# Rewriting the written order of a two-layer convolution kernel, with the first pair's norms taken chunk by chunk

## The chip, the cores and the metric

The kernel runs on one core of a Trainium2 chip. The metric is the device time of one execution in microseconds (us), the median of several runs.

## What is computed

Two layers act on an image `x` of shape (4, 128, 128, 128): 4 images, 128 channels, 128 x 128 pixels. Cut to what matters:

```python
def _block(x, ...):                       # t: one row of 128 channels for each pixel
    t = _ln(t, ln0_g, ln0_b)
    y1 = _ln(t, ln1_g, ln1_b)
    t = t + einsum(sigmoid(y1) * y1, W_out)
    y2 = _ln(t, ln2_g, ln2_b)
    wht = einsum(y2, W_whiten)
    k = square(relu(einsum(wht, W_key)))  # 512 hidden channels
    kv = einsum(k, W_value)
    r = sigmoid(einsum(wht, W_recep))
    return t + r * kv

x = x + _block(_gn(x)) + transposed(_block(transposed(_gn(x))))   # layer 0
x = x + conv3x3(_gn(x), weight[0]) + bias, scaled by a gate per channel   # layer 1
```

The block works on each pixel by itself, so its two calls give the same, and the kernel computes it once and adds it twice. `_gn` is a group norm over 4 channels and a whole image, `_ln` a layer norm over the 128 channels of a pixel. The gate of layer 1 comes from the mean of each channel of the normed image.

## The kernel before

**Tiling.** Channels lie on the 128 partitions. An image is cut into 32 chunks of 512 pixels; two chunks are a pair (16 pairs an image, 64 in all), four chunks a block of 16 rows (8 blocks an image, 32 in all). Twelve blocks are held in SBUF, and both layers write into them in place.

**Layer 0, one pair.** Each step is a word in the order, with the norm or chunk in its digits. In the names below `h` is the chunk of the pair, `j` the quarter of the hidden channels:

- `u` (L674, ACT) applies the group norm, `Tu` (PE) turns a chunk so that pixels lie on the partitions, 4 tiles of 128 x 128.
- `bn0h` (L685, DVE) takes the statistics of 4 tiles, `nb0` (L727) makes 1/std and -mean/std of them for all 8 tiles of the pair: six small steps, a power of -0.5 (L718, always on POOL) and two small steps. `t` (L735, ACT) applies them. `g` and `b` (L740, L744, POOL) are gain and shift.
- `bn1h`, `nb1`, `z1h` (ACT), `Tz1h` (PE) are the second norm and its way back to channels on partitions; `silu` (ACT), `att` (PE, 4 matmuls a chunk), and `T` (DVE) add the attention term to `t`.
- `bn2h`, `nb2` give the third norm's 1/std. `rc` (L771, DVE) turns it, `W` (L777) stores it in DRAM with four DMAs, `R` (L783) loads it for a chunk, spread over all partitions. `tt` (PE) turns `t` back and `cp` (L797, DVE) multiplies it with `R`.
- `pk` (L808, PE), `re` (ACT), `sq` (ACT, or DVE where the table FIRST_SQUARES has a D; from PSUM then), and `kv` (PE) are key, relu, square and value for `j` = 0 to 3; `pr`, `th` (ACT) the receptance; `q` (DVE) and `x` (POOL) gate and add, `S` (DVE) adds `t`, `bx` (DVE) takes the statistics for layer 1.

The power and the small steps belong to three words: `sa` the six steps, `pw` the power, `nb` the rest. For pairs under EARLY (2) the list has all three, with the small steps on DVE; for the others `nb` issues everything on POOL.

**Layer 1, one block.** The convolution is done by rows in a form with six products (`c0` to `c5`, L872, three matmuls each): DVE makes their inputs (`p`, `q`, `p2`, `q2`, `v0a` to `v5b`), and DVE and ACT combine the results (`e1`, `e3` on ACT; `a`, `b`, `c`, `d`, `ca`, `d8`, `y0` to `y3` on DVE). Up to the last image the six products share one PSUM bank ("conv", one buffer, L948), so that a product waits until the one before has been read. For the last image they have five tags of banks, of two or one buffers each, which layer 0 no longer needs. The weights of an image need the statistics of layer 0's output over the whole image (`conv_setup`, L498: statistics, seven small matmuls, a power, then the scaling), and a `*` in a list takes its next step.

**The order.** Every engine runs its instructions in the order in which they are written, and the words of the lists set it for all engines at once:

- FILL (L37): pairs 0 to 5, until the pipeline is full
- FIRST (L66): one list for each of the slots 6 to 16, layer 0 alone; `pk11:4` in slot s means pair s - 4
- HANDOVER (L80): layer 1 begins on image 0
- ORDER (L25): one list for each of the 21 slots 23 to 30, 39 to 46, 55 to 59, layer 0 of one pair beside layer 1 of the image before, a block in two slots (words in the set ODD in one, in EVEN in the other)
- BOUND (L143): the change from one image to the next, twice
- END (L210): the last four pairs and the last image's layer 1; pairs and blocks are counted from the end

Key banks (L801) are taken in turn: two of "h" and, before layer 1 begins, every third one of "conv".

Of the kernel before, what the change touches and what calls it, by code (L numbers as in the profile page):

```python
# [13 lines left out]
P = 128  # L14
# [11 lines left out]
    u1:0 Tu1:0 u0:0 x11:3 Tz10:1 Tu0:0 bn01:0 bn00:0 z11:1 bx1:3 v1:1 pr0:2 Tz11:1 q2:1  # L26
    silu0:1 p2:1 re00:2 sq00:2 y2:1 ca:1 att0:1 silu1:1 c0:1 pk01:2 nb0:0 d8:1 kv00:2 T0:1
    y0:1 th0:2 t1:0 bn20:1 v3:1 tt1:2 g1:0 re01:2 in0:0 c1:1 cp1:2 e1:1 att1:1 pk02:2 c3:1
    T1:1 bn21:1 pk10:2 c5:1 b1:0 y3:1 re02:2 S1:2 t0:0 nb2:1 e3:1 pk03:2 v2:1 g0:0 b0:0
    re10:2 c2:1 in1:0 a:1 pk12:2 sq01:2 sq10:2 v0a:1 sq02:2 re03:2 sq03:2 re12:2 b:1 kv01:2  # L30
    kv02:2 rc:1 pk13:2 re13:2 v4:1 pk11:2 kv03:2 sq12:2 c4:0 bn11:0 v5a:0 tt0:1 bn10:0 v0b:1
    pr1:2 q0:2 c:0 d:0 re11:2 sq11:2 S0:1 sq13:2 kv10:2 v5b:0 kv11:2 th1:2 kv12:2 kv13:2
    nb1:0 W:1 y1:0 R0:1 z10:0 q:0 cp0:1 pk00:1 R1:1 x10:2 p:0 bx0:2 q1:2
"""


FILL = """  # L37
    fetch:16 u1:0 u0:0 Tu1:0 bn01:0 u0:1 Tu0:0 u1:1 bn00:0 sa0:0 in1:16 pw0:0 in0:16
    fetch:17 nb0:0 t1:0 t0:0 Tu0:1 g1:0 bn00:1 b1:0 u1:2 Tu1:1 in1:17 g0:0 u0:2 in0:17
    bn11:0 fetch:18 b0:0 bn01:1 sa0:1 bn10:0 pw0:1 sa1:0 nb0:1 pw1:0 in1:18 t0:1 in0:18  # L40
    nb1:0 fetch:19 t1:1 Tu1:2 g0:1 bn01:2 b0:1 z10:0 Tu0:2 bn00:2 g1:1 z11:0 Tz10:0 b1:1
    in0:19 silu0:0 Tz11:0 bn10:1 nb0:2 u0:3 att0:0 in1:19 silu1:0 bn11:1 fetch:20 u1:3
    att1:0 sa1:1 T0:0 bn20:0 pw1:1 t0:2 T1:0 t1:2 bn21:0 g0:2 sa2:0 Tu0:3 nb1:1 pw2:0 Tu1:3
    in1:20 u1:4 in0:20 z10:1 g1:2 bn00:3 fetch:21 z11:1 bn01:3 nb2:0 b0:2 Tz10:1 rc:0 nb0:3
    W:0 silu0:1 Tz11:1 att0:1 silu1:1 in1:21 bn10:2 R0:0 att1:1 in0:21 b1:2 t0:3 T0:1
    fetch:22 T1:1 tt0:0 t1:3 g0:3 bn11:2 R1:0 tt1:0 Tu1:4 nb1:2 cp0:0 u0:4 bn20:1 u0:5 Tu0:4
    pk02:0 in1:22 S1:0 u1:5 bn01:4 pk00:0 re02:0 pk01:0 re00:0 g1:3 cp1:0 pk03:0 z10:2
    sq00:0 b1:3 bn00:4 pk11:0 re01:0 b0:3 re03:0 pr0:0 in0:22 z11:2 bn21:1 fetch:23 kv00:0
    nb0:4 pk10:0 S0:0 sq01:0 bn10:3 Tz10:2 re11:0 kv01:0 silu0:2 sa2:1 pk12:0 re10:0 bn11:3
    att0:2 sq02:0 pw2:1 sq03:0 kv02:0 T0:2 th0:0 nb2:1 nb1:3 Tz11:2 t1:4 rc:1 kv03:0 sq10:0  # L50
    W:1 pk13:0 q0:0 silu1:2 Tu1:5 in0:23 re12:0 att1:2 bn20:2 t0:4 R0:1 pr1:0 g1:4 bn01:5
    kv10:0 sq11:0 R1:1 x10:0 T1:2 Tu0:5 sq12:0 kv11:0 z10:3 bn00:5 tt1:1 tt0:1 nb0:5 kv12:0
    th1:0 cp0:1 re13:0 pr0:1 sq13:0 cp1:1 pk03:1 z11:3 S1:1 pk00:1 bn21:2 th0:1 kv13:0 g0:4
    S0:1 re00:1 Tz11:3 bx0:0 pk01:1 re03:1 b1:4 sq00:1 silu1:3 pk02:1 b0:4 bn11:4 re01:1
    Tz10:3 att1:3 re02:1 nb2:2 bn10:4 silu0:3 pk12:1 q1:0 pk10:1 re12:1 T1:3 att0:3 sq03:1
    bn21:3 sq01:1 kv00:1 nb1:4 re10:1 pk11:1 sq02:1 rc:2 sq10:1 W:2 pk13:1 re11:1 T0:3
    kv01:1 sq11:1 bn20:3 t1:5 kv02:1 x11:0 R0:2 kv03:1 sq12:1 nb2:3 tt0:2 q0:1 re13:1 R1:2
    pr1:1 bx1:0 t0:5 kv10:1 S0:2 kv11:1 sq13:1 kv12:1 x10:1 z10:4 cp0:2 tt1:2 pk01:2 g0:5
    S1:2 th1:1 pk00:2 cp1:2 re01:2 g1:5 pk03:2 re00:2 rc:3 kv13:1 sq00:2 re03:2 in1:23
    pk02:2 q1:1 pk10:2 bx0:1 x11:1 kv00:2 Tz10:4 bx1:1  # L60
# [3 lines left out]
EARLY = 2  # L64

FIRST = """  # L66
    u1:0 u0:0 Tu1:0 pk11:4 re02:4 pr0:4 z11:2 Tu0:0 in1:0 re10:4 silu0:2 Tz11:2 sq01:4
    bn01:0 W:3 att0:2 b1:1 sq10:4 bn00:0 R0:3 T0:2 th0:4 silu1:2 re11:4 kv01:4 b0:1 pk12:4
    sq03:4 tt0:3 bn10:1 sq02:4 pk13:4 sq11:4 cp0:3 re12:4 pr1:4 att1:2 th1:4 kv02:4 re13:4
    kv03:4 nb0:0 bn11:1 bn20:2 T1:2 S0:3 pk01:3 pk00:3 pk03:3 bn21:2 tt1:3 t0:0 q0:4 kv10:4  # L70
    nb1:1 sq12:4 kv11:4 re01:3 re00:3 sq13:4 in0:0 nb2:2 S1:3 kv12:4 sq00:3 kv13:4 R1:3
    x10:4 cp1:3 pk02:3 rc:2 q1:4 bx0:4 t1:0 x11:4 g1:0 z10:1 bx1:4 pk10:3 kv00:3 Tz10:1 g0:0
    re03:3
# [7 lines left out]
    load load load fetch:32 sq01:13 W:14 z11:15 re02:13 Tz11:15 R0:14 silu0:15 kv01:13 u1:17  # L81
    att0:15 R1:14 silu1:15 b0:16 pk11:13 T0:15 re10:13 att1:15 bn20:15 b1:16 u0:17 pk13:13
    re11:13 T1:15 Tu1:17 * bn21:15 tt0:14 re13:13 pr1:13 sq03:13 sq10:13 nb2:15 pr0:13
    sq02:13 bn01:17 u1:18 Tu0:17 pk12:13 bn00:17 sq11:13 kv02:13 th0:13 bn10:16 nb0:17
    sq13:13 tt1:14 kv03:13 th1:13 cp0:14 re12:13 q0:13 pk00:14 u0:18 bn11:16 kv10:13 sq12:13
    re00:14 pk01:14 cp1:14 x10:13 t1:17 S1:14 kv11:13 sq00:14 pk03:14 nb1:16 S0:14 t0:17
    Tu1:18 kv12:13 re01:14 pk12:14 bn01:18 re03:14 Tu0:18 u0:19 pk02:14 bn00:18 g0:17
    kv13:13 z10:16 rc:15 W:15 g1:17 tt0:15 q1:13 pk10:14 sq03:14 S0:15 sq01:14 nb0:18
    kv00:14 * re12:14 kv01:14 * re02:14 R0:15 * re10:14 pr0:14 bx0:13 sq02:14 R1:15 sq10:14
    pk11:14 sq12:14 Tz10:16 th0:14 b0:17 kv02:14 t1:18 kv03:14 x11:13 cp0:15 pk13:14 re11:14  # L90
    bn10:17 b1:17 t0:18 pk00:15 q0:14 pr1:14 bn11:17 sq11:14 x10:14 Tu0:19 * tt1:15 kv10:14
    * * nb1:17 th1:14 * kv11:14 re00:15 * kv12:14 cp1:15 re13:14 bn00:19 silu0:16 pk02:15
    sq13:14 sq00:15 re02:15 kv13:14 g0:18 S1:15 u1:19 pr1:15 q1:14 z11:16 b0:18 att0:16
    bx0:14 pk01:15 x11:14 z10:17 Tu1:19 Tz11:16 g1:18 bn01:19 pk03:15 th1:15 silu1:16
    kv00:15 T0:16 nb0:19 re01:15 bn20:16 pr0:15 z11:17 att1:16 bn10:18 re03:15 in1:32
    Tz11:17 pk10:15 sq01:15 T1:16 b1:18 sq03:15 bn21:16 Tz10:17 kv01:15 re10:15 nb2:16
    sq02:15 sq10:15 pk11:15 silu1:17 bx1:14 kv02:15 th0:15 kv03:15 silu0:17 t0:19 q0:15
    att0:17 rc:16 x10:15 bn11:18 W:16 pk12:15 re11:15 bx1:13 tt0:16 nb1:18 sq11:15 pk13:15
    T0:17 u0:20 bx0:15 t1:19 R0:16 Tu0:20 bn20:17 kv10:15 kv11:15 R1:16 re12:15 S0:16
    re13:15 att1:17 bn00:20 g0:19 sq12:15 sq13:15 kv12:15 g1:19 * kv13:15 cp0:16 u1:20 *  # L100
    b1:19 u1:21 Tu1:20 q1:15 pk01:16 z10:18 bn01:20 x11:15 pk00:16 nb0:20 re01:16 bx1:15
    Tz10:18 pr0:16 re00:16 T1:17 sq00:16 * tt1:16 silu0:18 bn21:17 * th0:16 att0:18 sq01:16
    cp1:16 nb2:17 t0:20 * pk10:16 p:0 bn11:19 pk11:16 t1:20 pk03:16 S1:16 * T0:18 b0:19
    re10:16 kv00:16 * rc:17 re03:16 in0:32 kv01:16 W:17 g1:20 re11:16 bn10:19 Tu1:21 z11:18
    pk02:16 b1:20 bn01:21 pk12:16 R0:17 re02:16 nb1:19 * Tz11:18 bn11:20 sq02:16 tt0:17
    u0:21 kv02:16 fetch:33 S0:17 sq03:16 bn20:18 * Tu0:21 re12:16 R1:17 pk13:16 * sq10:16
    bn00:21 kv03:16 g0:20 silu1:18 cp0:17 pr1:16 z11:19 q0:16 b0:20 att1:18 sq11:16 kv10:16
    * T1:18 sq12:16 nb0:21 tt1:17 * in0:33 re13:16 kv11:16 in1:33 th1:16 pk00:17 S1:17
    fetch:34 sq13:16 * z10:19 kv12:16 * bn10:20 * * re00:17 kv13:16 bn21:18 nb1:20 * Tz10:19
    * t0:21 cp1:17 pk01:17 in0:34 Tz11:19 pk02:17 re01:17 * * silu1:19 pk10:17 * q:0  # L110
    silu0:19 nb2:18 pr0:17 q2:0 sq00:17 att1:19 * re10:17 att0:19 t1:21 T1:19 pk03:17 q1:16
    x10:16 sq01:17 kv00:17 rc:18 bn21:19 re02:17 W:18 g1:21 kv01:17 sq02:17 T0:19 pk12:17
    th0:17 g0:21 in1:34 re03:17 kv02:17 bn20:19 x11:16 R0:18 sq03:17 tt0:18 z10:20 pk11:17
    S0:18 b0:21 kv03:17 * bx0:16 sq10:17 pk13:17 nb2:19 q0:17 re12:17 Tz10:20 * re11:17
    kv10:17 z11:20 cp0:18 pr1:17 * pk00:18 * sq11:17 b1:21 bn10:21 Tz11:20 re13:17 kv11:17
    silu0:20 p2:0 pk02:18 re00:18 v3:0 silu1:20 pk01:18 v1:0 th1:17 rc:19 att1:20 bn11:21
    W:19 re02:18 att0:20 * re01:18 nb1:21 T1:20 c1:0 sq01:18 bn21:20 u0:22 R1:19 T0:20 u1:22
    bn20:20 R0:19 tt0:19 e1:0 Tu1:22 tt1:18 x10:17 sq02:18 bn01:22 c3:0 R1:18 z11:21 nb2:20
    * fetch:35 sq13:17 sq12:17 Tu0:22 pr0:18 sq00:18 bn00:22 e3:0 pk03:18 th0:18 v4:0 nb0:22
    kv12:17 * cp1:18 kv13:17 re03:18 cp0:19 pk11:18 q1:17 pk10:18 in0:35 re11:18 in1:35 c4:0  # L120
# [161 lines left out]
def conv_preact_kernel(  # L282
# [358 lines left out]


    S = {}
    keys = [0]

    def flat(t):
        return t.rearrange("p s c -> p (s c)")
# [538 lines left out]
```

## Time and profile before

| What | us |
|---|---|
| median of 3 runs (1869.79 to 1872.17) | 1870.11 |
| the profiled execution | 1872.87 |
| its span, first to last instruction | 1871.1 |
| PE busy (97%) | 1806.3 |
| DVE busy (72%) | 1348.0 |
| ACT busy (68%) | 1269.8 |
| POOL busy (62%) | 1164.7 |
| mean granted PE clock | 0.996 |

PE is TensorE, DVE VectorE, ACT ScalarE, POOL GpSimd, SP the engine that issues most DMAs. In the page's rows of 40 slices a digit is the busy share of a slice in tenths. A line of the timeline or of a group has the start and the duration in us, the engine, the line of the kernel, the operation, the tile written and the tiles read, the shape and how many, and in brackets how long the engine was idle before it and what ended that. In the table by stage, the columns are the stage, its length, and for each of PE, PEld (weight loads), DVE, ACT and POOL the busy time and the number of instructions, then the granted clock, the DMA share and GB/s.

### The profile page before, as it was taken

What the parts mean: (1) busy time and instruction counts of PE and PEld (TensorE: products, weight loads), DVE (VectorE), ACT (ScalarE), POOL (GpSimd) and SP (SyncE); (2) the same over time, 40 slices, a digit from 0 to 9 for tenths busy, and PEclk for the clock granted to TensorE, in tenths of its full rate; (3) what the DMA queues carried; (4) which work ended last, traced back from release to release, by engine and by line L of the source; (5) the groups of instructions that cost most, each with busy time, mean ns of one, the idle gap of its engine ahead of it and who ended that gap; (6) DMA issues with size and microseconds to landing.
All of it is one profiled execution on the core that took longest, in us unless ns stands there. A gap on an engine that the chain in (4) does not pass through costs nothing.

```text
span 1871.1 us, 21825 instructions
## 1 busy us (share of the span) xinstructions
PE 1806.3 (97%) x6096; PEld 942.6 (50%) x6096; DVE 1348.0 (72%) x3336; ACT 1269.8 (68%) x2493; POOL 1164.7 (62%) x1915
## 2 busy tenths in 40 slices
PE   3799999999999999999999999999999999999999
PEld 2555555555545555455455455455455555554443
DVE  6767766677677677777757677777766667676987
ACT  2889899898666776777667777677766777753000
POOL 2878888887366666886556666788555667641211
PEclk9899999999999999999999999999999999999999
DMA  5211112221212212222112212211201111111112
GB/s 219 89 46 57 46 49 96 73 71 58 71 59 85 91 68 103 84 87 96 42 68 91 77 50 77 75 63 68 81 12 68 68 57 68 50 39 45 52 68 90
DMA packets 46072, 133.57 MB, mean 71 GB/s; under 512 B 8679, under 2 KB 15102, under 8 KB 38014
## 3 DMA queue, kind: packets, MB, share of 16 engines
q1 hardware_dynamic: 45504, 131.77, 20.5%
q8 instruction: 49, 0.80, 0.2%
q14 instruction: 73, 0.60, 0.1%
q10 hardware_dynamic: 446, 0.40, 0.1%
HBM read 97.14 MB, written 35.00 MB: 71 GB/s over the span
## 4 chain that ended last, share of the span: by engine, by line
PE 84%; DVE 5%; POOL 5%; DMA 3%; ACT 2%; issue 1%; SPq 0%; DVEq 0%; POOLq 0%
PE kv L837 21%; PE pk L810 21%; PE m L875 8%; PE m L877 8%; PE m L876 8%; PE pr L828 5%; PE att L763 5%; PE tt L659 3%; PE ut L659 3%; PE z1t L659 3%; DMA x<-in_x 1%; POOL rs L718 1%; DMA R<-rd 1%; DVE st L690 1%; ACT t L666 1%
## 5 line engine op out<-in xcount | busy, mean ns | idle before, releaser
L810 PE MATMUL pk<-y,wk_s 128*128 128x512 f32 x1024 | 503.3, 594 | 1.6 <-ACT h L814 0.9
L837 PE MATMUL kv<-h,wv 128*128 128x512 f32 x1024 | 492.7, 593 | 0.0
L814 ACT ACTIVATE h<-pk,kbias 128x512 f32<-128x512 f32 x512 | 349.3, 687 | 188.1 <-PE pk L810 178.3
L857 POOL TENSOR_TENSOR x<-x,r 128x512 f32<-128x512 f32 x128 | 166.7, 1302 | 202.4 <-DVE r L853 193.2
L837 PEld LDWEIGHTS kv<-h,wv 128*128 128x128 f32 x1024 | 187.1, 190 | 201.9 <-issue 177.2
L820 ACT ACTIVATE h<-h 128x512 f32<-128x512 f32 x480 | 286.5, 629 | 3.4
L810 PEld LDWEIGHTS pk<-y,wk_s 128*128 128x128 f32 x1024 | 183.0, 191 | 185.2 <-issue 148.0
L666 ACT ACTIVATE t<-ut,nb,rs 128x128 f32<-128x128 f32 x512 | 191.4, 466 | 90.6 <-POOL nb L725 82.7
L690 DVE BATCH_NORM_STATS2 st<-t 128x6 f32<-128x128 f32 x1024 | 219.0, 278 | 30.5 <-POOL t L746 28.7
L666 ACT ACTIVATE z<-t,nb,rs 128x128 f32<-128x128 f32 x512 | 209.5, 489 | 17.5 <-POOL nb L725 17.1
L718 POOL TENSOR_TENSOR rs<-rs,nhalf 128x8 f32<-128x8 f32 x128 | 215.4, 1682 | 6.0 <-DVE rs L711 6.0
L742 POOL TENSOR_TENSOR t<-t,g 128x512 f32<-128x512 f32 x128 | 163.8, 1285 | 74.7 <-ACT t L666 74.3
L875 PE MATMUL m<-v,u 128*128 128x512 f32 x384 | 198.5, 598 | 10.4 <-DVE v L899 5.0
L877 PE MATMUL m<-v,u 128*128 128x508 f32 x384 | 195.7, 591 | 0.0
L876 PE MATMUL m<-v,u 128*128 128x508 f32 x384 | 195.5, 591 | 0.0
L746 POOL TENSOR_TENSOR t<-t,b 128x512 f32<-128x512 f32 x128 | 166.0, 1304 | 5.6
L853 DVE SCALAR_TENSOR_TENSOR r<-r,kv 128x512 f32<-128x512 f32 x128 | 87.0, 680 | 86.2 <-PE kv L837 83.4
L763 PEld LDWEIGHTS att<-wo,y 128*128 128x128 f32 x1024 | 131.9, 196 | 31.5 <-issue 22.4
L767 DVE TENSOR_TENSOR t<-att,t 128x512 f32<-128x512 f32 x128 | 87.7, 685 | 78.3 <-PE att L763 77.8
L690 DVE BATCH_NORM_STATS2 st<-ut 128x6 f32<-128x128 f32 x512 | 112.3, 283 | 40.4 <-PE ut L659 39.8
L763 PE MATMUL att<-wo,y 128*128 128x128 f32 x1024 | 138.0, 280 | 0.8 <-DVE t L767 0.4
L828 PE MATMUL pr<-y,wr_s 128*128 128x512 f32 x256 | 130.7, 594 | 0.9 <-DVE h L824 0.7
(164 smaller groups left out, 2491.2 us busy)
## 6 DMA issues: line engine op xcount, KB each, us to landing
R<-rd SPq DMA_DIRECT2D x128, 256.0 KB
x<-in_x SPq DMA_DIRECT2D x31, 1024.0 KB
out<-x SPq DMA_DIRECT2D x31, 1024.0 KB
xs<-in_x SPq DMA_DIRECT2D x48, 512.0 KB
rd<-rrow SPq DMA_DIRECT2D x256, 1.0 KB
u<-raw SPq DMA_DIRECT2D x18, 192.0 KB
raw<-u SPq DMA_DIRECT2D x6, 192.0 KB
x<-in_x SPq DMA_DIRECT2D x2, 512.0 KB
```

Source lines behind the costliest of these rows:

```text
L666: nc.scalar.activation(dst[:, s, :], src[:, s, :], AF.Identity, bias=nb[:, i : i + 1], scale=rs[:, i : i + 1],)
L690: nc.vector.bn_stats(st[:, h * SUB + s, :], src[:, s, :])
L718: nc.gpsimd.tensor_tensor(rs, rs, nhalf, ALU.pow)
L763: nc.tensor.matmul(att[:, ts(s, P)], y[:, ts(s, P)], wo, start=True, stop=True)
L810: nc.tensor.matmul(pk, wk_s[:, ts(j, P)], S["y2", g, h], start=True, stop=True)
L814: nc.scalar.activation(k, S["pk", g, h, j], AF.Relu, bias=kbias[:, j : j + 1])
L820: nc.scalar.activation(k, k, AF.Square)
L828: nc.tensor.matmul(pr, wr_s, S["y2", g, h], start=True, stop=True)
L837: nc.tensor.matmul(S["kv", g, h], wv[:, j, :], S.pop(("h", g, h, j)), start=(j == 0), stop=(j == NH - 1))
L875: nc.tensor.matmul(pc, u[:, 1], v, start=True, stop=False)
L876: nc.tensor.matmul(pc[:, :, 1:W], u[:, 0], v[:, :, 0 : W - 1], start=False, stop=False)
L877: nc.tensor.matmul(pc[:, :, 0 : W - 1], u[:, 2], v[:, :, 1:W], start=False, stop=True)
```

## The change

It replaces all lists by others with nearly the same words, and changes the code in four places:

- Norms of pairs under EARLY, now 1 instead of 2, are taken chunk by chunk: `sa`, `pw` and `nb` have a second digit for the chunk and work on 4 columns instead of 8. Pair 1's norms are now whole `nb` words, on POOL.
- Pair 0's third norm is not stored in DRAM. `Rm` spreads it with four matmuls a chunk into a key bank, and a new step `Rc` copies that to SBUF on ACT. (The step `Rm` was in the code before, and no list used it.)
- FIRST_SQUARES has one more square on DVE.
- Key banks begin their turn at 1 instead of 0. A switch EARLY_GAIN is added and is 0.

In the new ORDER, `pk`, `re`, `sq` and `kv` of a pair stand mostly three slots behind its first step, where they stood two or one behind.

The diff, with the lists cut to what is spoken of below:

```diff
 ORDER = """
-    u1:0 Tu1:0 u0:0 x11:3 Tz10:1 Tu0:0 bn01:0 bn00:0 z11:1 bx1:3 v1:1 pr0:2 Tz11:1 q2:1
...
-    pr1:2 q0:2 c:0 d:0 re11:2 sq11:2 S0:1 sq13:2 kv10:2 v5b:0 kv11:2 th1:2 kv12:2 kv13:2
-    nb1:0 W:1 y1:0 R0:1 z10:0 q:0 cp0:1 pk00:1 R1:1 x10:2 p:0 bx0:2 q1:2
+    u1:0 p:1 kv00:3 u0:0 z10:1 sq02:3 Tu0:0 kv01:3 Tu1:0 kv02:3 re03:3 d:1 bn00:0 rc:2
+    Tz10:1 bn01:0 c2:2 in1:0 re12:3 z11:1 pk11:3 nb0:0 sq03:3 Tz11:1 a:2 silu0:1 sq10:3 W:2
+    sq12:3 re11:3 kv03:3 silu1:1 t0:0 R0:2 sq11:3 q2:1 q:1 tt0:2 t1:0 pk13:3 pr1:3 v3:1 c3:1
+    q0:3 re13:3 th1:3 att1:1 v4:1 b:2 g0:0 v1:1 e3:1 v5a:0 kv10:3 S0:2 cp0:2 att0:1 b0:0
...
 FILL = """
-    fetch:16 u1:0 u0:0 Tu1:0 bn01:0 u0:1 Tu0:0 u1:1 bn00:0 sa0:0 in1:16 pw0:0 in0:16
-    fetch:17 nb0:0 t1:0 t0:0 Tu0:1 g1:0 bn00:1 b1:0 u1:2 Tu1:1 in1:17 g0:0 u0:2 in0:17
-    bn11:0 fetch:18 b0:0 bn01:1 sa0:1 bn10:0 pw0:1 sa1:0 nb0:1 pw1:0 in1:18 t0:1 in0:18
...
+    fetch:16 u0:0 u1:0 Tu0:0 bn00:0 u0:1 Tu1:0 sa00:0 bn01:0 pw00:0 nb00:0 sa01:0 t0:0
+    in0:16 pw01:0 u1:1 in1:16 Tu0:1 g0:0 nb01:0 fetch:17 t1:0 bn00:1 b0:0 u0:2 Tu1:1 g1:0
+    bn10:0 u1:2 sa10:0 b1:0 bn01:1 pw10:0 in1:17 nb0:1 in0:17 nb10:0 fetch:18 bn11:0 z10:0
+    sa11:0 Tz10:0 pw11:0 t0:1 in1:18 t1:1 Tu0:2 g0:1 in0:18 bn00:2 fetch:19 b0:1 silu0:0
+    Tu1:2 nb11:0 att0:0 g1:1 bn01:2 z11:0 bn10:1 b1:1 Tz11:0 T0:0 nb0:2 silu1:0 bn20:0 u1:3
+    att1:0 sa20:0 u0:3 bn11:1 tt0:0 in1:19 pw20:0 t0:2 T1:0 in0:19 nb20:0 nb1:1 Rm0:0 S0:0
+    t1:2 fetch:20 bn21:0 Tu0:3 Rc0:0 Tu1:3 cp0:0 bn00:3 pk01:0 g0:2 z10:1 pk00:0 in1:20 g1:2
+    in0:20 z11:1 Tz10:1 bn01:3 fetch:21 b1:2 re01:0 Tz11:1 b0:2 u1:4 bn11:2 pk02:0 re00:0
+    nb0:3 silu0:1 sq00:0 bn10:2 silu1:1 att0:1 re02:0 in1:21 sq02:0 pr0:0 T0:1 sq01:0 kv00:0
+    in0:21 nb1:2 t0:3 att1:1 fetch:22 pk03:0 T1:1 t1:3 kv01:0 sa21:0 kv02:0 bn20:1 u0:4
+    Tu1:4 g1:3 z10:2 bn21:1 Tu0:4 pw21:0 bn00:4 re03:0 Tz10:2 nb21:0 th0:0 b1:3 bn01:4 Rm1:0
+    silu0:2 nb2:1 bn11:3 z11:2 att0:2 in0:22 sq03:0 tt1:0 Rc1:0 T0:2 kv03:0 g0:3 cp1:0 u1:5
...
-EARLY = 2
+EARLY = 1
+EARLY_GAIN = 0
...
-FIRST_SQUARES = ("DAAA", "DAAA")
+FIRST_SQUARES = ("DAAA", "DDAA")
...
-    keys = [0]
+    keys = [EARLY * PAIR * 2 % 3]
...
     def bn(k, g, h):
-        if ("st", k, g) not in S:
-            S["st", k, g] = small.tile([P, N, 6], F32, tag=f"st{k}", name="st", bufs=2)
-        st, src = S["st", k, g], norm_source(k, g, h)
+        early = g < EARLY
+        key, n = ("st", k, g) + ((h,) if early else ()), SUB if early else N
+        if key not in S:
+            S[key] = small.tile([P, n, 6], F32, tag=f"st{k}{n}", name="st", bufs=2)
+        st, src = S[key], norm_source(k, g, h)
         for s in range(SUB):
-            nc.vector.bn_stats(st[:, h * SUB + s, :], src[:, s, :])
+            nc.vector.bn_stats(st[:, s if early else h * SUB + s, :], src[:, s, :])
...
-    def norm_root(k, g):
-        rs, _, _ = S["terms", k, g]
-        nc.gpsimd.tensor_tensor(rs, rs, nhalf, ALU.pow)
+    def norm_root(k, g, *h):
+        rs, _, _ = S["terms", k, g, *h]
+        nc.gpsimd.tensor_tensor(rs, rs, nhalf[:, : SUB if h else N], ALU.pow)
...
-    def norm_terms(k, g):
-        if g < EARLY:
-            norm_end(k, g, nc.vector)
+    def norm_terms(k, g, *h):
+        if h:
+            norm_end(k, g, nc.vector, *h)
         else:
             norm_start(k, g, nc.gpsimd)
             norm_root(k, g)
...
     def spread_on_pe(g, h):
-        rs, _ = S["norm", 2, g]
-        S["R", g, h] = r = key_bank(g, "R")
+        rs, _ = S.pop(("norm", 2, g, h))
+        S["Rp", g, h] = r = key_bank(g, "R")
         for s in range(SUB):
-            i = h * SUB + s
             nc.tensor.matmul(
-                r[:, ts(s, P)], rs[:, i : i + 1].to_broadcast([P, P]), ident, start=True, stop=True
+                r[:, ts(s, P)], rs[:, s : s + 1].to_broadcast([P, P]), ident, start=True, stop=True
             )
+
+    def copy_spread(g, h):
+        S["R", g, h] = r = wk.tile([P, CH], F32, tag="R", name="R", bufs=3)
+        nc.scalar.copy(r, S.pop(("Rp", g, h)))
```

In END, after pair 63's last value product `kv13` (here pairs and blocks are written with their own numbers, `*` is a step of the weights' setup), the list before has

```
kv13:63 y3:22 bx1:62 v1:23 * c1:23 q1:63 x10:63 x11:63 bx1:63 bx0:63 v3:23 * e1:23 v2:23 v0a:23 * * * c3:23
```

then c2 and c4 of block 23 and c1 of block 24. The list after has

```
kv13:63 q1:63 x11:63 b:22 y2:22 bx0:62 ca:22 p2:23 bx1:63 * c0:22 y0:22 y1:22 v3:23 d8:22 * * * * * c5:22 y3:22
```

then c3, c1, c4 and c2 of block 23 and c1 of block 24.

## The prediction

> **What bounds the kernel now.** I read the busy times first, then the table by stage, then the waits of PE, then the two places where PE is idle longest. The page:
>
> ```profile
> PE 1806.3 (97%) x6096; PEld 942.6 (50%) x6096; DVE 1348.0 (72%) x3336; ACT 1269.8 (68%) x2493; POOL 1164.7 (62%) x1915
> PE   3799999999999999999999999999999999999999
> POOL 2878888887366666886556666788555667641211
> ```
>
> PE is the bound everywhere but in the first two slices, where POOL is nearly full. So an order can win only where PE is idle. How much that is I count from PE's timeline, start to start: a 512-column matmul (two records) takes 0.858 us, four transposed tiles 0.436, one attention chunk 0.893, one convolution product (six records) 2.567. 64 pairs x (18 x 0.858 + 2 x 0.893 + 6 x 0.436) + 192 x 2.567 = 1762.6 us of work. The first transposition starts at 34.6. Cutting the timeline where the lists end gives the idle time of each stage: FILL 31.95, the eleven FIRST slots 0.9, HANDOVER 6.0, the 21 ORDER slots 8.3 (4.1 of it in the first, slot 23), BOUND 6.8 and 6.6, END 13.0 (4.2 of it after the last product). 34.6 + 1762.6 + 73.6 is the span, 1871. The stage table (PE, PEld, DVE, ACT, POOL):
>
> ```profile
> 34.60:121.50 86.90, 68.96 (x256) 41.55 (x257) 63.46 (x215) 68.54 (x144) 70.00 (x108) 0.94 0.22 65
> 121.50:340.70 219.20, 219.20 (x842) 122.23 (x841) 152.55 (x430) 197.70 (x397) 178.45 (x330) 1.00 0.21 67
> ```
>
> In FILL no engine is full over the whole stage; in FIRST PE is full, ACT has 10% left. In FILL it is a chain through DVE, POOL, ACT and PE that sets the pace:
>
> ```profile
> 38.47 1.65 POOL L718 TENSOR_TENSOR rs<-rs,nhalf 128x8 f32<-128x8 f32 x1 [4.96 <-DVE rs L711]
> 41.92 1.12 PE L659 MATMUL ut<-ident,u 128*128 128x128 f32 x4 [5.34 <-ACT t L666]
> 51.87 1.11 PE L659 MATMUL ut<-ident,u 128*128 128x128 f32 x4 [7.44 <-ACT t L666]
> 62.32 0.66 PE L659 MATMUL ut<-ident,u 128*128 128x128 f32 x4 [1.65 <-ACT t L666]
> 76.29 4.57 PE L810 MATMUL pk<-y,wk_s 128*128 128x512 f32 x10
> ```
>
> PE waits for `t`, `t` for the norm, the norm for POOL's power. From 76.3 PE has key products and hardly stops. Later waits are single ones:
>
> ```profile
> 523.49 1.13 PE L875 MATMUL m<-v,u 128*128 128x512 f32 x2 [2.07 <-ACT e L951]
> 741.64 1.10 PE L875 MATMUL m<-v,u 128*128 128x512 f32 x2 [1.59 <-DVE v L899]
> 772.01 0.66 PE L659 MATMUL ut<-ident,u 128*128 128x128 f32 x4 [1.51 <-ACT t L666]
> 1726.21 0.38 PE L558 MATMUL pm<-mv,gmat 128*128 128x1 f32 x2 [1.90 <-DVE mv L555]
> ```
>
> **What the skill says.** The Trainium skill, "TensorE: Matmul & The Clock Gate", What's actually happening: an idle array runs at half clock until it has been busy for a while. The trace agrees: two attention chunks take 3.78 us at 68.61 and 1.79 later. "DMA: Bandwidth & Descriptors", Anatomy of one DMA: about 2 us fixed per transfer, measured there on GpSimd's queue; here, on SP's, the store of 1/std takes 2.60 us and the spreading load 3.50 (chain at 618), more than that with their data. "GPSIMD Engine Reference", Engine selection: two-input elementwise is about twice as slow as on VectorE; here 1.27 (L742) against 0.69 (L767).
>
> **The change, part by part.**
>
> FIRST. One more square (`sq11`) goes from ACT (0.63) to DVE (0.74). PE has no idle time there, ACT and DVE keep 10% and 27%. Cost 0; without that cover each slot would lose 0.1. The distance between a key bank's uses stays above what relu and square need.
>
> FILL, first chunk of pair 0. The chunk's own norm does not wait for the other chunk's statistics. bn 35.76 to 36.63, six DVE steps to 37.70, the power on 4 columns. That is not in the trace; 1 column takes 0.56 (L483), 8 take 1.65, so between these, in proportion 1.03: 38.63. DVE is in `bn01` until 38.64, then two steps; `t0` starts at 39.1, before at 40.36. The second chunk's `t` starts at 41.9 (before 41.8).
>
> FILL from there, walked down the new lists with the durations of the trace (POOL: gain or shift 1.28, a whole norm 3.7 as from 57.03 to 60.72, the third norm, which has three steps less, 3.1):
>
> - POOL: g0 41.05, b0, g1, b1 to 46.2; `pw10` 47.2; `nb0:1` (pair 1's norm, nine instructions which DVE shared before) 50.95; `pw11` 52.0; four gains and shifts 57.7; `nb0:2` 61.4; `pw20` 62.4; `nb1:1` 66.1.
> - z of pair 0 starts at 48.2 (before 53.07), its attention at 54.8 (56.99) and 58.0 (58.88), since `t` of pair 1 (51.1, before 50.31) stands ahead of its silu on ACT.
> - `Rm0` on PE 62.5, its copy behind `t` of pair 2 on ACT at 64.3 to 64.9, `cp0` 65.7: the first key product at 65.7, before at 76.29.
> - pair 1: z at 66.2 (64.70), attention at 72.4 (68.61); pair 2: attention at 82.7 (85.89).
> - chunk 1 of pair 0: `pw21` stands behind two norms and a gain, done at 80.9; `Rc1` behind `sq03` on ACT at 85.5; its key products at 87 (79.84).
>
> PE is full from about 88; before from 81. By 102.1 it has done, by the lists, 36.0 us of work and the two spreads; before 35.6. So the ten microseconds of the first key product are given back by pair 1 and by the second chunk. The spreads are 2 x 8 records like the attention's, 2 x 0.9 us, placed where PE waits: cost 0, 1.8 without that cover. `Rm1` waits on PE for `pw21` with pair 2's attention behind it, which waits for its silu at 82.7 anyway; `Rc0` has pair 1's z behind it on ACT, which waits for POOL at 66.1. The spreads save pair 0 the trip through DRAM (four stores and two loads off SP's queue). The copies are 2 x 0.58 on ACT. I take 0 for FILL, -4 to +4: the walk's end points differ by 0.4, its steps may be off by some us.
>
> POOL is why. By the lists of FILL it has 6 x 1.03 + 5 x 3.7 + 4 x 3.7 + 3 x 3.1 + 23 x 1.28 + 4 x 1.3 = 83 us; before 6 x 1.65 + 4 x 3.7 + 3 x 3.7 + 2 x 3.1 + 22 x 1.28 + 4 x 1.3 = 75.
>
> HANDOVER, ORDER, BOUND. Not PE's work changes but its distances. The lists of all engines are one list, so a step's place in it, as PE work written ahead of it, is the time that it was planned for if PE never stops. I took that distance between each producer and its consumer and set it against the producer's measured duration. What is missing, summed over the steps that stand over 0.4 us too close: HANDOVER 17.7 before, 11.3 now; an ORDER slot 24 and 8.5; a BOUND 82 and 52. The store of 1/std and its use (`W`, `cp0`) stood at distance 0 in ORDER, now at 4.8 or more; slots are 27.5 and 27.5 of work, not 30.1 and 25.0. Of the idle time, the setup's small matmuls are fixed (some 1.2 in HANDOVER, 2.1 in each BOUND). The rest: 4.8 + (3.8 + 1.5 in ORDER) + 4.7 + 4.5 = 19.3. A third to two thirds of the closeness is gone; I take half the idle time: -9.5. Bounds: 0 to -17, and +4 if new waits come (0.2 in each ORDER slot).
>
> END. After the last value product PE had c1, c3, c2, c4 of block 23, then c1 of block 24, whose weights need the output norm: 17.2 us from 1720.08 to 1737.26, for 11.1 us of products. Now it has c0, c5 of block 22 and c3, c1, c4, c2 of block 23, one after the other through one PSUM bank ("conv", one buffer), each waiting for its eviction: `q1` and `b` to 2.45, c0 to 5.1, y0 behind the statistics to 7.5, c5, y3 11.0, c3 and e3 14.5, c1 and e1 18.1, c4, c and d 22.3, c2, c1 of block 24 at 24.9. That is 7.7 us later for 5.1 us more work: +2.6. `W` of pairs 61 and 62 stands only 2 us ahead of `cp0`, against 6.1 for store and load, and DVE holds `T1` behind it. I take +2.5; bounds -4 and +5.
>
> Sum: 0 - 9.5 + 2.5 = -7 on a span of 1871.1. The profiled execution took 1872.87 with 1.77 around the span, the median of the runs is 1870.11; I take the difference off the median: **1863**.
>
> **Rivals.** (1) *The start pays.* The first key product is 10.6 us earlier; if pair 1 isn't late (a POOL norm nearer to 3 than 3.7), chunk 0's 9 matmuls, 7.7 us, go into time in which PE was idle. With the -9.5 and half the END's loss: 1854. For: 31 of FILL's 32 us of idle time lie before 76; against: POOL is full from 41 on. (2) *Slower: POOL carries the start.* Its 8 us more in FILL and pair 1's attention 3.8 later are both handed to PE: +11.8 + 2.5 - 9.5 = 1875. It decides once FILL's idle time passes 43 (before 32), which takes 10.8 off the forecast's lead. For: POOL waited only some 5 us between 57 and 121; against: FIRST leaves POOL 3.7 us a slot to catch up. (3) *No difference.* Waits taken out of HANDOVER and BOUND come back at other places, as END's bank: half of -9.5 and a FILL of +2: 1870.
>
> **Numbers.** About 0.2% (3.7 us) can be told from no change. Forecast (1858 to 1866) 0.46; start pays (below 1858) 0.18; no difference (1866.4 to 1873.9) 0.21; slower 0.15. Faster 0.64, same 0.21, slower 0.15. Range 1853 to 1875, with a tenth on each side.
>
> **What would show it.** First pk near 66, pk of chunk 1 of pair 0 near 87, PE full from 88; POOL with no gap from 41 to 121. FIRST slots at 19.86. ORDER slots at 27.6 each. HANDOVER and each BOUND with 3 to 4 us idle. From the last kv to c1 of block 24 some 25 us. I am wrong if FILL ends (first `ut` of pair 6) more than 4 us from its place, or if an ORDER slot takes over 27.8.

## The result and the profile after

| | us |
|---|---|
| median before, 4 runs (1869.79 to 1872.17) | 1870.28 |
| median after, 4 runs (1941.20 to 1946.47) | 1941.8 |
| ratio after / before, 95% interval | 1.0386 (1.0368 to 1.0404) |
| span of the profiled execution, before and after | 1871.1, 1940.5 |

The change made the kernel 3.9% slower. The prediction, 1863 with a range of 1853 to 1875, was wrong by far and in sign. The page of the kernel after, its busy times and two rows of slices (busy PE and granted clock):

```profile
PE 1824.5 (94%) x6112; PEld 948.2 (49%) x6112; DVE 1404.5 (72%) x3351; ACT 1263.0 (65%) x2479; POOL 1171.0 (60%) x1939
...
PE   3899999999899889999988988999999999999999
...
PEclk9999999999999999999989998999999999999999
```

The second digit of PE is now 8: the start isn't the loss. The 8s further on are: slices 11, 14 and 15 (of 48.5 us each) fall on the ORDER slots from 23 to 30, slices 21, 22, 24 and 25 in those from 39 to 46. With PE's idle time counted from its timeline as in the prediction, stage by stage (the forecast takes half of the idle time that could move in HANDOVER, ORDER and BOUND; the last column is the sixth experiment, which keeps these lists but gives the transfers and `in1` other places):

| idle PE, us | before | forecast | after | `e6` |
|---|---|---|---|---|
| FILL | 31.95 | 31.95 | 30.32 | 30.44 |
| FIRST, 11 slots | 0.9 | 0.9 | 1.6 | 1.6 |
| HANDOVER | 5.97 | 3.6 | 13.15 | 5.58 |
| ORDER, 21 slots | 8.3 | 5.6 | 74.8 | 0.2 |
| BOUND, two | 6.8, 6.6 | 4.4, 4.3 | 4.31, 4.19 | 9.54, 7.31 |
| END | 13.0 | 15.5 | 13.95 | 15.73 |

The stages of after against before give 68.8 us more idle time; with 1.8 for the spreads' matmuls and 1.3 off the first transposition (at 33.3, before 34.6) that is 69.3, and the spans differ by 69.4. So nearly all of it is in ORDER, and there it has a pattern. The table by stage of the kernel after, with FILL, ORDER slot 39 and slot 40:

```profile
33.30:119.50 86.20, 67.29 (x270) 40.50 (x271) 67.90 (x215) 68.61 (x144) 73.77 (x131) 0.98 0.18 56
985.10:1022.90 37.80, 30.51 (x96) 15.32 (x95) 24.47 (x55) 19.64 (x39) 20.77 (x34) 0.86 0.26 98
1022.90:1050.40 27.50, 27.50 (x95) 14.37 (x94) 21.25 (x47) 19.35 (x39) 17.17 (x30) 1.00 0.07 19
```

Slot 40 is full. Slot 39 has the same matmuls and takes 37.8, at a clock of 0.86. All even slots are like slot 40 (27.56 with 0.01 idle). The eight odd slots from 23 to 45, in which a block of 1 MB is loaded and two chunks of the next image are fetched, lose 7.6 to 10.2 us each. Slots 55, 57 and 59 load a block too, but have no chunk left to fetch: 55 loses 2.4, 57 and 59 at most 0.12. So the load alone is not what costs most. What PE waits for in slot 39, and what DVE waits for before that:

```profile
992.47 1.02 PE L843 MATMUL pr<-y,wr_s 128*128 128x512 f32 x2
1000.78 2.08 PE L890 MATMUL m<-v,u 128*128 128x512 f32 x2 [7.29 <-DVE v L914]
1002.65 1.90 PE L891 MATMUL m<-v,u 128*128 128x508 f32 x2
```

```profile
985.32 0.69 DVE L988 TENSOR_TENSOR x<-m,e 128x512 f32<-128x512 f32 x1 [0.16 <-PE m L892]
...
995.74 0.69 DVE L1019 BATCH_NORM_STATS2 st<-xs 128x6 f32<-128x512 f32 x1 [6.85 <-DMA xs<-in_x]
996.35 1.04 DVE L928 TENSOR_TENSOR q<-x 128x512 f32<-128x512 f32 x1
997.31 1.75 DVE L914 SCALAR_TENSOR_TENSOR q<-x 128x512 f32<-128x512 f32 x1
998.98 1.75 DVE L914 SCALAR_TENSOR_TENSOR v<-q,p 128x512 f32<-128x512 f32 x1
```

```profile
996.79 1.72 POOL L752 TENSOR_TENSOR t<-t,g 128x512 f32<-128x512 f32 x1
```

PE waits 7.29 us for `v`, the input of a convolution product. DVE would have made it, but stands 6.85 us at `in1` (L1019), the statistics of a chunk of the next image, for the chunk to arrive. The three steps behind it, up to `v`, then take 1.04, 1.75 and 1.75 us; in experiment 1, where DVE reaches them earlier, they take some 0.7 each. The late ones run beside POOL's gain and shift (`g`, `b`), which are slow as well (1.72 for 1.28). That is 2.5 us more of delay. After its wait PE runs at half clock (0.50 granted): the product takes 5.25 us, from 1000.78 to 1006.03, instead of 2.57. 7.29 and 2.7 are the 10.0 of the slot's 10.2. Why the chunk is late stands in SP's queue. First after, slot 39 (it begins at 985.1); then before, slot 41 (it begins at 1020.3):

```profile
986.10 0.34 SPq L1001 DMA_DIRECT2D out<-x  x1
989.96 0.33 SPq L363 DMA_DIRECT2D x<-in_x  x1
990.35 0.43 SPq L1013 DMA_DIRECT2D xs<-in_x  x1
990.82 1.47 SPq L793 DMA_DIRECT2D rd<-rrow  x4
996.40 0.82 SPq L798 DMA_DIRECT2D R<-rd  x2
```

```profile
1009.68 0.34 SPq L986 DMA_DIRECT2D out<-x  x1
1010.92 2.12 SPq L781 DMA_DIRECT2D rd<-rrow  x4
1014.39 0.82 SPq L786 DMA_DIRECT2D R<-rd  x2
1015.32 0.36 SPq L358 DMA_DIRECT2D x<-in_x  x1
1015.72 0.43 SPq L998 DMA_DIRECT2D xs<-in_x  x1
```

The five rows are the same five transfers: the store of a finished block, the load of a new one, the fetch of the chunks for `in0` and `in1`, and the store and load of 1/std. The block load waits for the block store, since it takes the stored block's buffer. Before, the store went out 10.6 us ahead of its slot, load and fetch some 5 us ahead, and `in1` stood in mid-slot: the statistics ran at 1027.16 and 1032.37, 11 us and more after the fetch was issued. After, `y3`, the block's last row, stands at the end of the even slot (DVE at 985.32), so the store leaves at 986.10, in the odd slot; the load waits 3.9 us for it; the fetch is issued behind the load, and the 1/std store behind that. `in1` is now the 18th word of the slot: DVE reaches it at 988.9, before its fetch has even been issued (990.35), and the data lands 5.4 us after that, beside 1 MB. The small stores of 1/std take 5.6 us from 990.82 to the load that needs them; in slot 40 the same four take 2.3. The lists of waits over the whole kernel, of DVE and of SP, after:

```profile
DVE st L1019 <- DMA xs<-in_x: 66.6, 19, 7.7
...
DVE y L814 <- DMA R<-rd: 20.9, 8, 6.3
```

```profile
SPq L363 <- DMA out<-x: 70.4, 20, 4.0
```

Of the first, 50.1 us lie in the eight ORDER slots. Before, it was 4.1 us in 4 waits and the last 26.1 in 9. HANDOVER has the same fault twice. Its `fetch:32` is written behind three block loads:

```profile
350.90 1.29 DVE L1019 BATCH_NORM_STATS2 st<-xs 128x6 f32<-128x512 f32 x2 [4.26 <-DMA xs<-in_x]
```

and until 393.05 ACT stands 4.53 us for the convolution's weights (L530), whose loads were issued at 389.34 and which the list uses at once.

### The profile page after: what moved, and what is told of

The parts are those of the page before. It is cut to its first block, busy times and chain, and to the rows that moved or that the text cites. A ratio compares the mean times of both kernels' runs of the same rounds, so it can differ in the third digit from the quotient of the medians.

```text
span 1940.5 us, 21926 instructions
## 1 busy us (share of the span) xinstructions
PE 1824.5 (94%) x6112; PEld 948.2 (49%) x6112; DVE 1404.5 (72%) x3351; ACT 1263.0 (65%) x2479; POOL 1171.0 (60%) x1939
## 4 chain that ended last, share of the span: by engine, by line
PE 80%; DVE 8%; DMA 7%; POOL 2%; issue 1%; ACT 1%; SPq 0%; DVEq 0%
PE pk L825 20%; PE kv L852 19%; PE m L890 8%; PE m L891 8%; PE m L892 8%; PE att L774 5%; PE pr L843 5%; DMA xs<-in_x 3%; PE tt L664 2%; PE z1t L664 2%; DMA out<-x 2%; PE ut L664 2%; DMA x<-in_x 2%; DVE st L696 1%; DVE st L1019 1%
## 5 line engine op out<-in xcount | busy, mean ns | idle before, releaser
L825 PE MATMUL pk<-y,wk_s 128*128 128x512 f32 x1024 | 512.0, 598 | 10.3 <-ACT r L847 7.0
L852 PE MATMUL kv<-h,wv 128*128 128x512 f32 x1024 | 508.1, 594 | 0.5 <-ACT h L835 0.5
L890 PE MATMUL m<-v,u 128*128 128x512 f32 x384 | 205.6, 618 | 56.7 <-DVE v L914 51.3
L852 PEld LDWEIGHTS kv<-h,wv 128*128 128x128 f32 x1024 | 178.5, 191 | 145.4 <-issue 136.0
L872 POOL TENSOR_TENSOR x<-x,r 128x512 f32<-128x512 f32 x128 | 175.0, 1368 | 108.1 <-DVE r L868 107.6
L725 POOL TENSOR_TENSOR rs<-rs,nhalf 128x8 f32<-128x8 f32 (+1 forms) x132 | 214.8, 1627 | 5.4 <-DVE rs L718 5.4
L891 PE MATMUL m<-v,u 128*128 128x508 f32 x384 | 201.4, 607 | 0.0
L892 PE MATMUL m<-v,u 128*128 128x508 f32 x384 | 199.7, 602 | 0.0
L714 POOL TENSOR_TENSOR rs<-st 128x8 f32<-128x8 f32 x126 | 37.8, 300 | 239.3 <-DVE st L696 239.2
L757 POOL TENSOR_TENSOR t<-t,b 128x512 f32<-128x512 f32 x128 | 176.0, 1377 | 6.7
L778 DVE TENSOR_TENSOR t<-att,t 128x512 f32<-128x512 f32 x128 | 87.6, 686 | 82.7 <-PE att L774 74.5
L890 PEld LDWEIGHTS m<-v,u 128*128 128x128 f32 x384 | 71.0, 195 | 137.4 <-issue 70.2
```

Of the source, the lines that this page charges most:

```text
L725: nc.gpsimd.tensor_tensor(rs, rs, nhalf[:, : SUB if h else N], ALU.pow)
L757: eng.tensor_tensor(t, t, over(b0), ALU.add)
L825: nc.tensor.matmul(pk, wk_s[:, ts(j, P)], S["y2", g, h], start=True, stop=True)
L852: nc.tensor.matmul(S["kv", g, h], wv[:, j, :], S.pop(("h", g, h, j)), start=(j == 0), stop=(j == NH - 1))
L890: nc.tensor.matmul(pc, u[:, 1], v, start=True, stop=False)
L891: nc.tensor.matmul(pc[:, :, 1:W], u[:, 0], v[:, :, 0 : W - 1], start=False, stop=False)
```

## The experiments

The theory to begin with: DVE stands at `in1`, which the new ORDER uses early while its fetch comes late; with `in1` back at its place the loss goes, and in the kernel before, where the fetch is early, an early `in1` does little harm. The rivals: SP's queue as a whole is late, and with `in1` out of the way its next consumer waits instead, `cp` with the spread 1/std; the load's place in the queue alone does it; or the loss belongs to the denser lists as such, whatever the transfers do. The expectations, written before each run, name some of them by letters.

**1. `in1` late again** (after, otherwise unchanged).

```diff
-    Tz10:1 bn01:0 c2:2 in1:0 re12:3 z11:1 pk11:3 nb0:0 sq03:3 Tz11:1 a:2 silu0:1 sq10:3 W:2
+    Tz10:1 bn01:0 c2:2 re12:3 z11:1 pk11:3 nb0:0 sq03:3 Tz11:1 a:2 silu0:1 sq10:3 W:2
...
-    bx1:3 re10:2 in0:0 c4:0 pk12:2 c:0 nb2:1 y3:1 S1:2 p2:0 pk03:2 v2:1
+    bx1:3 re10:2 in1:0 in0:0 c4:0 pk12:2 c:0 nb2:1 y3:1 S1:2 p2:0 pk03:2 v2:1
```

> One word of the changed ORDER moved: the statistics in1 of the next image's input go from the 17th place of the slot to the place ahead of in0, late in the slot. Theory A (DVE stands at in1 for a fetch that SP issues late, behind the block's load, which waits for a block's store): odd slots fall from 35 to 38 us to about 27.6, the kernel from 1941.8 to 1870 to 1880. Theory B (1/std, stored and spread behind the same load, comes too late for cp): DVE only waits at another place, odd slots stay above 33, the kernel above 1920. Theory C (no transfer: DVE has too much to do ahead of v3 for c3): odd slots stay where they are, 1935 to 1942.

Measured 1909.9 us, ratio 1.020 (1.0183 to 1.0218): half of the loss is gone. ORDER's idle time falls from 74.8 to 37.8. In slot 39 SP and DVE show who waits now:

```profile
973.07 1.50 SPq L793 DMA_DIRECT2D rd<-rrow  x4
979.03 0.82 SPq L798 DMA_DIRECT2D R<-rd  x2
```

```profile
982.15 0.69 DVE L814 TENSOR_TENSOR y<-tt,R 128x512 f32<-128x512 f32 x1 [5.16 <-DMA R<-rd]
```

The queue is as it was, with load and fetch ahead of these two, and DVE now stands 5.16 us at `cp` (L814) for 1/std, 63.9 us in the whole kernel (20.9 in after). The result lies between the theory and its rival: the place of `in1` is one cause, and behind it waits the next consumer of the same queue.

**2. The fetch ahead of the load** (after; in `slot`, the block load is issued behind `fetch_stats`).

> The changed kernel with the lists untouched; in a slot the fetch of the input chunk is written ahead of the block's load instead of behind it, so only two neighbours on SP's queue change places, and in1 stays early. Theory A: the fetch no longer waits for the store, odd slots fall to about 28, the kernel to 1870 to 1885. Theory B: store and spread of 1/std stand behind the load as before, no gain, above 1925. Theory C: no change, 1935 to 1942.

Measured 1907.64 us, 1.0197 (1.0176 to 1.0218): again half. The fetch no longer waits for the store, and in the eight ORDER slots `in1` waits 1.7 to 3.3 us for it, where it waited 5.3 to 7.7. PE now waits 24.9 us for `cp`. The stores of 1/std are still behind the load, but in slot 39 they are not what comes last: DVE reaches `cp` at 993.26 and finds 1/std there. It is late by its 3.31 us at `in1` and by slow steps behind it, beside POOL, of the kind seen above. So this place of the fetch alone is not enough.

**3. The early place alone, in the kernel before.**

```diff
-    u1:0 Tu1:0 u0:0 x11:3 Tz10:1 Tu0:0 bn01:0 bn00:0 z11:1 bx1:3 v1:1 pr0:2 Tz11:1 q2:1
+    u1:0 Tu1:0 u0:0 x11:3 Tz10:1 Tu0:0 bn01:0 bn00:0 in1:0 z11:1 bx1:3 v1:1 pr0:2 Tz11:1 q2:1
...
-    re10:2 c2:1 in1:0 a:1 pk12:2 sq01:2 sq10:2 v0a:1 sq02:2 re03:2 sq03:2 re12:2 b:1 kv01:2
+    re10:2 c2:1 a:1 pk12:2 sq01:2 sq10:2 v0a:1 sq02:2 re03:2 sq03:2 re12:2 b:1 kv01:2
```

> The kernel before with one word of ORDER moved: in1 to the place early in the slot that it has in the changed ORDER. There the block's store is issued ten us before the slot and the fetch some 5 us before it. Theory A (early statistics and a late store together): at most 1 to 2 us in an odd slot, the kernel at 1870 to 1885. If the early place alone were the cause: 6 to 10 us in each odd slot, 1920 to 1945.

Measured 1875.51 us, 1.0023 (1.0015 to 1.0032), some 4 us. In slots 23 and 39, the first of their stages, the idle time rises by 3.0 and 2.5 us, more than the 1 to 2 expected; in the other odd slots by at most 0.8. With load and fetch 5 us ahead of the slot, as in the kernel before, an early `in1` costs little. Early use and late transfers together make the loss, not the early use.

**4. HANDOVER's transfers** (experiment 1, and in HANDOVER `fetch:32` ahead of the three loads; the weights' setup is interrupted once more behind its loads, by a `yield`, and takes one more `*`, so that the loads go out some words before their use).

> The first experiment's move, and in HANDOVER two transfers issued earlier: the fetch of input chunk 32 ahead of the three block loads instead of behind them, and the three loads of the convolution's weights by a step of their own some 30 us ahead of their first use. Theory A, the same thing at other places: HANDOVER's idle time falls from 13.2 to 4 us, so about 9 below the first experiment, 1861 to 1871. If HANDOVER's waits have another cause: as the first experiment.

Measured 1897.32 us, 1.0142 (1.012 to 1.0164). The level was missed, since it was built on a level for experiment 1 that did not come; against experiment 1 it is 12.6 us less. HANDOVER's idle time goes from 11.56 to 6.79. The rest of the difference lies in ORDER (37.8 to 31.0), for which the edit gives no reason that was tried.

**5. The load late** (after; only the block load moves, from the slot's start to behind the word `R1`, so that fetch, 1/std store and 1/std load are issued ahead of it).

```diff
-        if s % 2 and s + 1 >= NP and len(blocks) < B * NBLK:
-            load_block(len(blocks))
+        pending = s % 2 and s + 1 >= NP and len(blocks) < B * NBLK
...
+            if op == "R1" and pending:
+                load_block(len(blocks))
+                pending = False
```

> The changed kernel, lists untouched; in an odd slot the block's load is written behind the two loads that spread 1/std instead of at the slot's start. The half of the loss that the first two experiments each left is put down to the same load: it holds SP until a store has landed, and its 1 MB then lies ahead of the small stores of 1/std on the DMA engines. Theory D (the load is the only cause of both waits): in1 and cp no longer wait, odd slots at 27.6 to 28.5, the kernel at 1868 to 1880. Theory B' (1/std is late for cp because store and use stand too close, load or not): odd slots stay at 30 to 34 as in the first experiment, about 1905.

Measured 1906.38 us, 1.0196 (1.018 to 1.0211): half once more. That is the level which theory B' named, but its reason is not there: in the eight slots DVE waits nowhere for 1/std. `in1` waits 1.7 to 3.4 us, now because the fetch is issued, right behind the 1 MB store, at the start of the slot in which it is used, and the steps behind it fall beside POOL's gain and shift again. Slot 39:

```profile
978.29 0.69 DVE L1019 BATCH_NORM_STATS2 st<-xs 128x6 f32<-128x512 f32 x1 [3.44 <-DMA xs<-in_x]
...
985.61 1.34 DVE L952 TENSOR_TENSOR v<-x,x 128x128 f32<-128x128 f32 x1
...
988.68 0.67 DVE L814 TENSOR_TENSOR y<-tt,R 128x512 f32<-128x512 f32 x1
```

The five steps from 981.29 to 988.08 take 6.8 us. In experiment 6, where `in1` stands behind them, the same five take 2.1, and L952 0.28. Slots 55, 57 and 59, which have no `in1`, lose nothing any more (55 lost 2.4). The load's place is the other cause, and alone it isn't enough either.

**6. All transfers** (experiments 4 and 5 together, with two of HANDOVER's three loads moved behind `R1:14`).

> All moves of transfers together: late in1, HANDOVER's early fetch and weights, two of HANDOVER's three block loads behind the spreading loads, and the block's load of a slot behind them too. Theory D: 31 us below the fourth experiment for the odd slots and 2 for HANDOVER, 1860 to 1868, below the kernel before. Theory B': above 1890.

Measured 1869.36 us over 12 runs, 0.9994 (0.9985 to 1.0002). The level is a little above the 1860 to 1868 expected, and far below theory B' (above 1890). The ORDER slots take 27.56 with at most 0.09 us idle. SP's queue in slot 41 (it begins at 1005.8):

```profile
1006.03 0.34 SPq L1002 DMA_DIRECT2D out<-x  x1
1006.42 0.43 SPq L1014 DMA_DIRECT2D xs<-in_x  x1
1008.71 1.59 SPq L794 DMA_DIRECT2D rd<-rrow  x4
1013.42 0.82 SPq L799 DMA_DIRECT2D R<-rd  x2
1014.29 0.42 SPq L363 DMA_DIRECT2D x<-in_x  x1
```

The store still leaves in the odd slot, but SP no longer waits for its landing ahead of the small transfers; the load comes last, when its buffer is long free. But for `in1` and a step of the weights' setup the engines' own order is that of the kernel after. So the denser lists as such lose nothing in ORDER, and the 72 us between the two kernels lie in where transfers are issued and used.

**7. END's banks** (experiment 6; block 23, the last one before the last image, may use the five tags of banks as the last image does).

```diff
-            where = ("kv", "tr", "tr", "ut", "ut", "conv")[i] if ending else "conv"
+            where = ("kv", "tr", "tr", "ut", "ut", "conv")[i] if ending or k == (B - 1) * NBLK - 1 else "conv"
```

> The sixth experiment, and the products of block 23, which come after the last value product, use the five tags of banks of the last image instead of the one conv bank. If the single bank is what makes the END's crossing 25.7 us long: 2 to 4 us below the sixth. If DVE's queue is: 0 to 1.

Measured 1867.26 us, 0.9982 (0.9975 to 0.9989), 2.1 below experiment 6. END's idle time falls from 15.73 to 12.14; from the last value product to c1 of block 24 it takes 24.5 us instead of 27.5. Of these 3.0 us, 1.7 are not the bank's: in the profiled execution of experiment 6 one product there (c5 of block 22) runs partly at half clock and takes 4.37 us, and in those of after and of experiment 10, with the same list and the one bank, it doesn't, and the stretch takes 25.76. The one bank was a part of END's loss, 1.3 us by this count, not all of it.

**8. Gains of the first pair on DVE** (experiment 6 with EARLY_GAIN = 1).

> The sixth experiment with the switch EARLY_GAIN at 1: pair 0's gains and shifts, four instructions of 1.28 us on POOL, are done by DVE in 0.7 each. If POOL paces FILL from 41 us on, FILL gets 1 to 5 us shorter and the kernel with it. If not: within 1 us of the sixth.

Measured 1867.07 us, 0.9986 (0.9979 to 0.9993), 2.3 below experiment 6. FILL's idle time falls from 30.44 to 29.05; where the rest comes from is open. POOL's load in FILL has a price, but a small one.

**9. What was found, together** (6, 7 and 8, and `u` of a pair that needs a fresh block moved behind work that doesn't: `u0:18` behind `re10:13` in HANDOVER, `u0:2` behind `th1:-3` in BOUND, where ACT had stood 3.35 us at `u` for a block load).

> The sixth, seventh and eighth experiments together, and one word moved in HANDOVER and one in each BOUND: u0 of the pair whose block is still being loaded goes behind the tanh th1, which ACT held up by 3.4 us while it waited for that load. If waits of a queue's head for a late transfer are what is left in these stages: HANDOVER at 4 us of idle time, the BOUNDs some 1.8 lower each, the kernel at 1858 to 1863, below the kernel before by 0.4 to 0.6%. If not: about 1865, the sum of the seventh and eighth.

Measured 1859.38 us over 5 runs beside 1870.65 of the kernel before: 0.9941 (0.9928 to 0.9955), 0.6% faster. HANDOVER's idle time is 4.99, the two BOUNDs' 7.07 and 3.93, END's 12.15. In both BOUNDs the wait of PE behind that `u`, 1.67 and 1.57 us in experiment 6, is gone. What else is lower there than in experiment 6 isn't settled, since experiment 10, without this move, is lower too. On the page PE is busy in all slices but the first two.

**10. The square back on ACT** (experiment 6 with FIRST_SQUARES as before; one run).

> The sixth experiment with FIRST_SQUARES as before, one square less on DVE in a FIRST slot. The slots took 19.93 us with the new table and 19.86 in the kernel before. If the square on DVE is the reason: 19.86 again, 0.8 us in all. If it is the list: 19.93 still, or more, as ACT then has 0.63 us more.

Measured 1864.22 us. The FIRST slots take 19.93 as they do with the added square, so the 0.07 a slot is the list's, not the square's. The BOUNDs have 6.76 and 5.86 us idle here, against 9.54 and 7.31 in experiment 6, though FIRST comes long before them. A single run doesn't settle why.

## Why the prediction was wrong

**HANDOVER, ORDER, BOUND: the step that failed.** The prediction measured "that distance between each producer and its consumer", and among these producers it counted the compute steps and the store of 1/std. It took SP's queue to be free. The fetch has no word of its own in ORDER; it is issued at the slot's start behind the block load, and so has no distance in such a count. That `in1` was moved from mid-slot to the 18th place was in the diff, and that the load waits for a store which `y3` releases was in the code; neither was walked. The bound "+4 if new waits come (0.2 in each ORDER slot)" was set for all slots alike by nothing measured; it came to 7.6 to 10.2 us in each of eight slots, 72.3 in these, and ORDER's idle time rose by 66.5. The prediction's own sign of being wrong, an ORDER slot over 27.8, is met in all eight. Two consequences of a wait were not priced and made it worse: of slot 39's 10.2 us, 2.7 are PE at half clock after it, and 2.5 of DVE's delay come from steps that fell beside POOL's work. The distance of 4.8 us between `W` and `cp0` was also taken as enough, though the prediction itself has 6.1 for store and load: even in experiment 6 DVE waits 1.1 to 2.1 us at `cp` in seven of the eight slots, where PE has the slack for it.

HANDOVER lost 7.2 where 2.4 was to be won, by the same thing. Experiments 1, 2 and 5 each remove one part of the cause and each get about half of the loss back; 6 removes all parts and gets everything back.

**Half of the closeness, half of the idle time: partly right.** With the transfers out of the way (experiment 6), ORDER's idle time is 0.2, a gain of 8.1 where 2.65 was forecast: the distance of the lists does pay there, more than was taken. HANDOVER gains 0.4 for 2.4. The BOUNDs lose 2.7 and 0.7 for a forecast gain of 2.35 and 2.25. In the kernel after they have 4.31 and 4.19, as forecast, but with PE held back in the slots ahead of them, so that is no proof for the lists; experiments 6, 9 and 10 give 9.5, 7.1, 6.8 for the first with the same BOUND list but for one word. What sets it stays open. The three come to -5.1 instead of -9.5.

**FILL: right.** The walk held at its own steps (first `t` of pair 0, and first key product, after):

```profile
37.57 1.50 ACT L670 ACTIVATE t<-ut,nb,rs 128x128 f32<-128x128 f32 x4 [2.25 <-DVE nb L734]
```

```profile
65.85 1.99 PE L825 MATMUL pk<-y,wk_s 128*128 128x512 f32 x4 [0.53 <-DVE y L814]
```

After, the first transposition comes 1.3 us earlier than before (33.3 for 34.6), which the forecast's times don't contain. With 1.3 added, `t0` starts at 38.9 (forecast 39.1), the first key product at 67.2 (65.7), pair 1's attention at 73.3 (72.4), pair 2's at 83.3 (82.7) and the key products of pair 0's second chunk at 87.6 (87). The power on 4 columns takes 1.02, as the proportion gave. FILL is 86.2 long, before 86.9: the ten microseconds of the first key product are given back, as the walk said. POOL was not without a gap, as the prediction's signs had it: it waited 1.64 us at 43.57 and 0.65 at 52.79. The rival "POOL carries the start" did not occur: the kernel is slower, as that rival has it, but by another mechanism and in another stage.

**END: the path right, its cost too high.** From the last value product to c1 of block 24 it took 25.75, for a forecast of 24.9 and 17.2 before. The forecast cost of 2.5 is 0.95 in after. In experiment 6 it is 2.7, but 1.7 of that is the stretch at half clock told above; so the agreement with 2.5 there is luck. Experiment 7 shows the bank as the reason of a part of it.

**FIRST: nearly.** 0 forecast, 0.07 a slot measured, 0.7 in all, and not by the square (experiment 10).

## What to carry to other kernels

An order that is made from the durations of the engines' instructions must hold the DMA issues too: where each is written, what its queue waits for ahead of it (here a load for a store), and how long it takes to land behind large ones. For each word that consumes a transfer, find the word that issues it and the last word that the queue must wait for, and price the distance; a transfer that is issued by the loop's frame, and not by a word, is the one that such a count overlooks. When a fix of one late transfer gives half of the loss back, look for the next consumer in the same queue, and for steps that the delay has moved beside another engine's work, before the theory is dropped.

## What the runs showed that was not expected

- A wait of PE costs more than its length. After 7.29 us of waiting, three matmuls of two records each took 5.25 us instead of 2.57; after 2.94 us in experiment 1, the attention chunk's records too took 2.04 instead of 1.05. The Trainium skill, "TensorE: Matmul & The Clock Gate", What's actually happening, says that an idle window, about 3.4 us by its table, puts the clock to half. The 7.29 us agree with it; the 2.94 us are shorter than such a window, and so is the wait of 1.87 us ahead of the slow product in experiment 6's END, so here the measurement goes further than the page. The same wait of 1.86 us in after left the clock at 1.00: whether a short wait is punished differs from execution to execution.
- DVE's steps that make the convolution's inputs are slow beside POOL's instructions on 128x512. In experiment 5, DVE's step L952 on 128x128 takes 0.28 us in the 17 cases where no such POOL instruction runs beside it, and 1.35 in the 11 where one does; the statistics of `in1` take 0.68 either way. A late DVE is made later by this. That POOL is the reason was not tried by itself.
- Four small stores of 1/std, issued behind a 1 MB load and a fetch on SP's queue, let the load that needs them go 5.6 us after the first was issued; 2.3 us in slot 40, where nothing large is just ahead. With the load out of the way but a 1 MB store and the fetch ahead of them, as in experiments 5 and 6, they still take 5.1 and 4.7 us (slots 39 and 41): moving the load let them start earlier more than it made them faster. The Trainium skill, "DMA: Bandwidth & Descriptors", Queues, rings and completion order, says that on each DMA engine descriptors are consumed in ring order, which fits; that this is the reason, and not the shared bandwidth, was not tried by itself.
